# Gather stage: ScalarE copies a tick's transposes one tick later, and the convolutions and biases follow

## The chip, the cores and the metric

The kernel runs on one core of a Trainium2 chip. The metric is device time in microseconds (us) from launch to end of one execution; lower is better. The times given are of three runs, and one more execution was recorded by the hardware profiler.

The core has five engines with a queue each, worked through in the order in which the program lists their instructions: TensorE (PE in the profile, its weight loads PEld), VectorE (DVE), ScalarE (ACT), GpSimd (POOL) and SyncE (SP). They meet only through semaphores: an instruction waits until another engine's counter has reached a value.

## What is computed

Four layers, each a residual around a normalised input, on x of shape (8, 128, 64, 64) in float32. Layer 0 is a state-space block, Layer 1 passes rows and columns along in four directions (63 steps each), Layer 2 multiplies two convolutions, Layer 3 is a deformable convolution. The change lies in Layer 3:

```python
def corner(yi, xi, wgt):
    valid = (yi >= 0) & (yi < H) & (xi >= 0) & (xi < W)
    idx = jnp.clip(yi, 0, H - 1) * W + jnp.clip(xi, 0, W - 1)
    g = jax.vmap(lambda xb, ib: xb[:, ib])(xf, idx)
    return g * (wgt * valid)[:, None]
samp = corner(y0, x0, (1 - wy1) * (1 - wx1)) + corner(y0, x0 + 1, (1 - wy1) * wx1) + corner(y0 + 1, x0, wy1 * (1 - wx1)) + corner(y0 + 1, x0 + 1, wy1 * wx1)
samp = samp * mask[:, None]
out = jnp.einsum('bckhw,ock->bohw', samp, dcn_w.reshape(COUT, C, KK))
out = out + dcn_b[None, :, None, None]
```

For each of the 9 taps of each pixel, four neighbours (all 128 channels) are read at computed places, weighed and summed; a product over channels and taps then gives 128 output channels. After that come a normalisation over the whole batch and a leaky ReLU.

## The kernel before

**Stages.** Layer 0 runs first, over all eight images, with Layer 1's first half batch beside it. Then comes one long loop over ticks (lines 116 to 131) that puts together what is left of Layer 1, all of Layer 2 and Layer 3's gather. `finish` normalises and writes the result at the end.

**The loop.** Its order is written out by hand. A tick lists, in this order: one Layer 1 step's nine products (`next(step)`, L724, while Layer 1 lasts), `three.tick` (the gather), the step's sum on VectorE (the second `next(step)`, L732), Layer 2's events that are due (`plans`), and pieces of the `ahead` threads (loads of x into X at L700 to L701, residual adds at L761 to L764). An image has 96 ticks. Image b of the gather runs beside Layer 2 of image b+1; the gather has 8 x 96 = 768 ticks.

**A gather tick** takes one tile of 128 pixels (t, 32 to an image) and three taps (k0 = 0, 3 or 6). `gather` lists

- three indirect DMAs on GpSimd (L1105), one a tap, which fetch for each of the 128 pixels one row of 4 x 128 values,
- on ScalarE six weighings in place (L1116: three taps, neighbours 2 and 3), each with the pixel's weight as scale; every twelfth tick a copy of other weights comes ahead of them (L1095), which waits for VectorE's previous tick,
- on VectorE the weighing of neighbours 0 and 1 (L1121) and the sums. With `halves` 1 (the first 324 ticks) the four neighbours become one (L1125 to L1127), with `halves` 2 (the other 444, where the rows land in Layer 1's old buffer X) they become two (L1123) and TensorE adds the rest.

Landing buffers: six with `halves` 1 (`got`), ten with `halves` 2 (parts of X). A gather's DMAs wait until the transposes of the gather six or ten ticks earlier have read their buffer.

**What follows a gather** goes through `later(ticks, f)`, which puts a call on a list for the tick n + ticks; `tick` runs its `gather` first and then that tick's list, in the order in which the calls were put there.

- `turn`, one tick later: TensorE transposes the sums, pixels by channels into channels by pixels, by products with the identity (L1137: three taps, one or two each) into a PSUM tile `ps_s` with two buffers; ScalarE copies the tile (L1140) into half of a `samp` tile. Two tiles of pixels share a `samp`, which has four buffers.
- `convolve`, two ticks after the second pixel tile of a pair: three products of 256 columns (L1148) that accumulate into `ps_o`, which has one buffer. After the third group of taps, ScalarE adds the bias into `o_out` (L1156), and every second time
- `store`, two ticks on: SP writes `o_out` to DRAM (L1161) and VectorE takes its statistics (L1162).

A tick's ScalarE queue therefore reads: weighings of gather n, bias if one is due, copy of the transposes of gather n-1, then what Layer 2 lists in that tick (the main ones: L866 and L883 around t1, L856 and L900, L951 for tokens, L983 and L993 for offsets). Its TensorE queue reads: Layer 1's step (L724), convolution of gather n-2, transposes of gather n-1, then Layer 2's products (L876, L890, L948, L972). Its VectorE queue reads: L1121 and the sums of gather n, statistics, L732, Layer 2's work (L905 to L909).

Of the kernel before, what the change touches and what calls it, by code (L numbers as in the profile page):

```python
# [17 lines left out]
P = 128  # L18
# [9 lines left out]
KK = 9  # L28
# [1039 lines left out]
class Layer3:  # L1068
# [21 lines left out]
    def gather(self, b, t, k0, idx, wgt, halves):  # L1090
        nc, G3 = self.nc, self.G3
        if k0 == 0 and t % self.WT == 0:
            self.wps = self.prod[:, t // self.WT % 2, self.G3 * C : self.G3 * C + self.WT * KK * 2]
            self.wps = self.wps.rearrange("p (t k q) -> p t k q", k=KK, q=2)
            nc.scalar.copy(self.wps, wgt[:, t : t + self.WT, :, 0:2])  # L1095
        if t % self.PAIR == 0:
            self.samp[k0] = self.w2.tile([P, G3, self.PAIR * P], F32, name="samp", bufs=4)
        if halves == 1:
            got = self.w2.tile([P, G3, 4, C], F32, name="got", bufs=6)
        else:  # L1100
            n = self.n % (HW * NB2 // (G3 * 4 * C))
            got = self.more[:, n * G3 * 4 * C : (n + 1) * G3 * 4 * C].rearrange("p (k q c) -> p k q c", k=G3, q=4)
        tab = self.tables[b]
        for k in range(G3):
            nc.gpsimd.indirect_dma_start(  # L1105
                out=got[:, k, :, :].rearrange("p q c -> p (q c)"),
                out_offset=None,
                in_=tab,
                in_offset=bass.IndirectOffsetOnAxis(ap=idx[:, t, k0 + k : k0 + k + 1], axis=0),
            )  # L1110

        for k in range(G3):
            for q in (2, 3):
                nc.scalar.activation(  # L1116
                    got[:, k, q, :], got[:, k, q, :], AF.Identity, scale=wgt[:, t, k0 + k, q : q + 1]
                )
        prod = self.prod[:, :, 0 : G3 * C].rearrange("p q (k c) -> p k q c", c=C)
        w = self.wps[:, t % self.WT, k0 : k0 + G3, :]  # L1120
        nc.vector.tensor_mul(prod, got[:, :, 0:2, :], w.unsqueeze(3).to_broadcast([P, G3, 2, C]))  # L1121
        if halves == 2:
            nc.vector.tensor_add(got[:, :, 0:2, :], prod, got[:, :, 2:4, :])  # L1123
        else:
            nc.vector.tensor_add(prod[:, :, 0, :], prod[:, :, 0, :], got[:, :, 2, :])  # L1125
            nc.vector.tensor_add(got[:, :, 1, :], prod[:, :, 1, :], got[:, :, 3, :])
            nc.vector.tensor_add(got[:, :, 0, :], prod[:, :, 0, :], got[:, :, 1, :])  # L1127
        self.later(1, self.turn, halves, got, self.samp[k0], t % self.PAIR * P)
        if t % self.PAIR == self.PAIR - 1:
            self.later(2, self.convolve, b, t + 1 - self.PAIR, k0, self.samp[k0])  # L1130

    def turn(self, halves, got, samp, col):
        nc = self.nc
        ps = self.pp.tile([P, self.G3, P], F32, name="ps_s")
        for k in range(self.G3):
            for q in range(halves):
                nc.tensor.matmul(  # L1137
                    ps[:, k, :], lhsT=got[:, k, q, :], rhs=self.ident, start=(q == 0), stop=(q == halves - 1)
                )
        nc.scalar.copy(samp[:, :, col : col + P], ps)  # L1140

    def convolve(self, b, t0, k0, samp):
        nc, N2 = self.nc, self.PAIR * P
        if k0 == 0:
            self.ps_o = self.pp.tile([P, N2], F32, name="ps_o", bufs=1)
        ps = self.ps_o
        for k in range(k0, k0 + self.G3):
            nc.tensor.matmul(  # L1148
                ps, lhsT=self.dcn_w[:, k, :], rhs=samp[:, k - k0, :], start=(k == 0), stop=(k == KK - 1)
            )  # L1150
        if k0 + self.G3 < KK:
            return
        if t0 % 4 == 0:
            self.out = self.w2.tile([P, T], F32, name="o_out")
        o = self.out[:, t0 % 4 * P : t0 % 4 * P + N2]
        nc.scalar.activation(o, ps, AF.Identity, bias=self.dcn_b)  # L1156
        if t0 % 4:
            self.later(2, self.store, b, t0 // 4, self.out)
# [99 lines left out]
```

## Time and profile before

| | us |
|---|---|
| median of three runs | 7638.51 (7635.89 to 7647.05) |
| profiled execution | 8068.85 |
| its span, first to last instruction | 8066.5 |
| first and last weighing of the gather stage (start) | 3749.8 and 7891.9 |
| last step of Layer 1 | 5364 |
| busy in the span: TensorE, VectorE, ScalarE, GpSimd | 6262.5, 4469.1, 3505.2, 4114.6 |
| mean granted TensorE clock | 0.889 of full speed |

The profiled execution took 430 us longer than the median run. Line numbers are those of the kernel shown above. In a row of the profile, `out<-in` are the program's names of tiles, `x768` the number of instructions, then busy time and mean duration in ns, then the idle time of that engine just before these instructions and what ended most of it. A releaser `DMA name` is a transfer that landed, `issue` is idle time with no wait that the profile can name, `remote` a semaphore for which no record of this program accounts. TensorE's matmul ends are modelled by the profiler. A float32 product shows as two matmul records, so a set of transposes is 6 records with `halves` 1 and 12 with `halves` 2, and a convolution's three products are 6.

### The profile page before, as it was taken

Reading aid. Unit: us, or ns where it says so; the run is one execution under the profiler, and the core shown is the slowest. Engines: PE = TensorE matmul, PEld = TensorE weight load, DVE = VectorE, ACT = ScalarE, POOL = GpSimd, SP = SyncE. Lnnn points to the kernel's source line nnn. Section 1 sums busy time; section 2 is a strip of 40 time slices with the busy share of each in tenths; the row PEclk is TensorE's granted clock in tenths of the full one; section 3 lists DMA queues with packets and bytes.
Section 4 is the critical chain, followed back from the end, with each engine's and each line's share of the span. In section 5 each row is a group of like instructions: output and inputs, shape, how many; then the busy total and the mean of one; then the engine's idle time right before and its main releaser. Section 6 shows DMA issues by size and latency. Waiting matters only on the chain. (4 is left out here: it accounts for less than half of the span.)

```text
span 8066.5 us, 87137 instructions
## 1 busy us (share of the span) xinstructions
PE 6262.5 (78%) x30226; PEld 4059.5 (50%) x30226; DVE 4469.1 (55%) x5384; ACT 3505.2 (43%) x8218; POOL 4114.6 (51%) x3325
## 2 busy tenths in 40 slices
PE   6777878799999999538999999974467777676661
PEld 1222222255555556416777777753355555555551
DVE  4887887666666655111556545555445454454445
ACT  4554555433333331021444444444355555555453
POOL 3766666544444443111445444445565666666664
PEclk9887888799999999869999999987689888888785
DMA  1010110100000000131455455455566666666557
GB/s 41 26 44 26 38 36 28 35 12 24 21 19 18 17 14 9 54 118 51 150 174 160 155 163 158 152 163 172 170 201 194 207 195 201 192 199 201 177 176 259
DMA packets 333015, 897.77 MB, mean 111 GB/s; under 512 B 55464, under 2 KB 90544, under 8 KB 330528
## 3 DMA queue, kind: packets, MB, share of 16 engines
q0 software_dynamic: 184320, 604.13, 24.7%
q1 hardware_dynamic: 143648, 271.31, 10.3%
q10 hardware_dynamic: 4608, 16.78, 0.5%
q8 instruction: 239, 3.92, 0.2%
q14 instruction: 200, 1.64, 0.1%
HBM read 770.80 MB, written 121.21 MB: 111 GB/s over the span
## 5 line engine op out<-in xcount | busy, mean ns | idle before, releaser
L605 POOL TENSOR_TENSOR hb<-hb,bc 128x1024 f32<-128x1024 f32 x512 | 1216.4, 2379 | 1360.9 <-ACT carry L600 979.1
L1105 POOL DMA_INDIRECT X<-table,idx x1332 | 1272.1, 955 | 799.8 <-PE ps_s L1137 350.1
L1105 POOL DMA_INDIRECT got<-table,idx x972 | 930.0, 957 | 1083.8 <-ACT samp L1140 439.8
L594 DVE TENSOR_TENSOR_SCAN hb<-da,carry,u_ps 128x512 f32<-128x512 f32 x896 | 1098.0, 1267 | 275.8 <-PE ps_y L613 224.7
L576 ACT ACTIVATE da<-dt_ps 128x1024 f32<-128x1024 f32 x512 | 524.3, 1024 | 1316.0 <-PE dt_ps L559 1315.6
L1148 PE MATMUL ps_o<-samp,dcn_w 128*128 128x256 f32 x2304 | 676.4, 436 | 418.7 <-ACT samp L1140 224.0
L1137 PE MATMUL ps_s<-ident,X 128*128 128x128 f32 x5328 | 794.9, 308 | 241.2 <-DVE X L1123 144.7
L1140 ACT COPY samp<-ps_s 128x384 f32<-128x384 f32 x768 | 365.1, 475 | 1412.6 <-PE ps_s L1137 1033.7
L1123 DVE TENSOR_TENSOR X<-prod,X 128x768 f32<-128x768 f32 x444 | 425.2, 958 | 966.1 <-ACT X L1116 805.6
L1137 PEld LDWEIGHTS ps_s<-ident,X 128*128 128x128 f32 x5328 | 767.3, 221 | 303.1 <-DVE X L1123 161.7
L1116 ACT ACTIVATE X<-X,wgt 128x128 f32<-128x128 f32 x2664 | 826.1, 392 | 0.0
L559 PE MATMUL u_ps<-u,m_u 32*128 32x512 f32 x2048 | 639.3, 703 | 194.4 <-DVE hb L594 193.4
L1148 PEld LDWEIGHTS ps_o<-samp,dcn_w 128*128 128x128 f32 x2304 | 470.2, 214 | 554.2 <-ACT samp L1140 251.2
L583 DVE TENSOR_TENSOR u_ps<-u_ps,bc 128x1024 f32<-128x1024 f32 x512 | 625.2, 1221 | 182.1 <-PE dt_ps L559 165.3
L1116 ACT ACTIVATE got<-got,wgt 128x128 f32<-128x128 f32 x1944 | 611.2, 392 | 193.6 <-DMA got<-table,idx 189.9
L559 PE MATMUL dt_ps<-dt,m_dt 32*128 32x512 f32 x2048 | 642.5, 706 | 17.6 <-ACT da L576 17.6
L1121 DVE TENSOR_TENSOR prod<-X,prod 128x768 f32<-128x768 f32 x444 | 426.5, 961 | 117.4 <-ACT prod L1095 69.3
L1125 DVE TENSOR_TENSOR prod<-prod,got 128x384 f32<-128x384 f32 x324 | 183.6, 567 | 506.3 <-ACT got L1116 453.7
L559 PEld LDWEIGHTS u_ps<-u,m_u 32*128 32x128 f32 x2048 | 166.3, 198 | 553.2 <-DVE hb L594 365.9
L1121 DVE TENSOR_TENSOR prod<-got,prod 128x768 f32<-128x768 f32 x324 | 309.6, 955 | 145.7 <-DMA got<-table,idx 96.0
L1137 PE MATMUL ps_s<-ident,got 128*128 128x128 f32 x1944 | 296.1, 293 | 109.5 <-issue 47.6
L876 PE MATMUL ps_t<-xn,w 128*128 128x512 f32 (+4 forms) x688 | 317.3, 611 | 81.1 <-DVE t L907 56.6
(224 smaller groups left out, 10218.1 us busy)
## 6 DMA issues: line engine op xcount, KB each, us to landing
x<-x1d SPq DMA_DIRECT2D x128, 256.0 KB
table<-tok SPq DMA_DIRECT2D x128, 256.0 KB
X<-table,idx POOLq DMA_INDIRECT x1332
x<-x2d SPq DMA_DIRECT2D x48, 384.0 KB
x3h<-x3d SPq DMA_DIRECT2D x16, 1056.0 KB
x_st<-in_x SPq DMA_DIRECT2D x64, 256.0 KB
x_o<-in_x SPq DMA_DIRECT2D x64, 256.0 KB
x1d<-res SPq DMA_DIRECT2D x64, 256.0 KB
```

The source lines that it names most:

```text
L559: nc.tensor.matmul(ps[:, j, :], lhsT=mask[q, r].rearrange("p d n -> p (d n)"), rhs=S[c][src, h][q, :], start=True, stop=True,)
L576: nc.scalar.activation(da, steps[i]["dt"], AF.Exp)
L583: nc.vector.tensor_mul(st["bc"], st["bc"], s["bc", h][:, 0].unsqueeze(1).to_broadcast([P, 2, T]))
L594: nc.vector.tensor_tensor_scan(hb[:, j, :], st["da"][:, j, :], st["bc"][:, j, :], start, ALU.mult, ALU.add)
L605: nc.gpsimd.tensor_mul(hb, hb, S[c]["bc", h][:, 1].unsqueeze(1).to_broadcast([P, 2, T]))
L1105: nc.gpsimd.indirect_dma_start(out=got[:, k, :, :].rearrange("p q c -> p (q c)"), out_offset=None, in_=tab, in_offset=bass.IndirectOffsetO ...
L1116: nc.scalar.activation(got[:, k, q, :], got[:, k, q, :], AF.Identity, scale=wgt[:, t, k0 + k, q : q + 1])
L1121: nc.vector.tensor_mul(prod, got[:, :, 0:2, :], w.unsqueeze(3).to_broadcast([P, G3, 2, C]))
L1123: nc.vector.tensor_add(got[:, :, 0:2, :], prod, got[:, :, 2:4, :])
L1137: nc.tensor.matmul(ps[:, k, :], lhsT=got[:, k, q, :], rhs=self.ident, start=(q == 0), stop=(q == halves - 1))
L1140: nc.scalar.copy(samp[:, :, col : col + P], ps)
L1148: nc.tensor.matmul(ps, lhsT=self.dcn_w[:, k, :], rhs=samp[:, k - k0, :], start=(k == 0), stop=(k == KK - 1))
```

## The change

Three calls are put one tick later than what they follow:

- the copy of the transposes leaves `turn` and goes on the list of the next tick,
- `convolve` is called three ticks after its gather, not two,
- the bias with what follows it becomes a function `biased`, called one tick after the last group's convolution; `store` still comes two ticks after the bias.

In tick n ScalarE then has the weighings of gather n, a bias if one is due, and the copy of the transposes of gather n-2; TensorE has the convolution of gather n-3 and the transposes of gather n-1. No instruction is added or left out, and no buffer count changes.

```diff
         if t % self.PAIR == self.PAIR - 1:
-            self.later(2, self.convolve, b, t + 1 - self.PAIR, k0, self.samp[k0])
+            self.later(3, self.convolve, b, t + 1 - self.PAIR, k0, self.samp[k0])
 
     def turn(self, halves, got, samp, col):
...
-        nc.scalar.copy(samp[:, :, col : col + P], ps)
+        self.later(1, nc.scalar.copy, samp[:, :, col : col + P], ps)
 
     def convolve(self, b, t0, k0, samp):
...
-        if k0 + self.G3 < KK:
-            return
+        if k0 + self.G3 == KK:
+            self.later(1, self.biased, b, t0, ps)
+
+    def biased(self, b, t0, ps):
+        nc, N2 = self.nc, self.PAIR * P
         if t0 % 4 == 0:
             self.out = self.w2.tile([P, T], F32, name="o_out")
```

In the changed kernel the copies carry the line of `later` (L1088), since it is there that the call is made, and bias, store and statistics stand three lines further down (L1159, L1164, L1165).

## The prediction

> **What bounds the kernel now.** I read the page first, then the busy times of four stretches, the waits of TensorE in the first of them, and two short timelines. The page names the group that the change moves: 768 copies of transposes out of PSUM, in front of which ScalarE stands idle, mostly for the transposes of line 1137.
>
> ```profile
> span 8066.5 us, 87137 instructions
> ...
> L1140 ACT COPY samp<-ps_s 128x384 f32<-128x384 f32 x768 | 365.1, 475 | 1412.6 <-PE ps_s L1137 1033.7
> ```
>
> Idle time of an engine that is not the bound is free, so the question is who waits for ScalarE. The gather runs from about 3750 to 7897 us, and its stretches have different limits (windows, all engines):
>
> ```profile
> 3850.00:5380.00 1530.00, 1417.88 (x7177) 1180.77 (x7175) 848.12 (x1433) 694.50 (x2027) 723.71 (x757) 0.98 0.51 158
> 5380.00:5840.00 460.00, 213.78 (x728) 150.36 (x728) 233.12 (x382) 179.44 (x507) 254.62 (x247) 0.69 0.57 178
> 5840.00:7500.00 1660.00, 1189.09 (x6579) 949.00 (x6580) 809.00 (x957) 939.50 (x2788) 1012.03 (x1059) 0.88 0.64 197
> 7500.00:7840.00 340.00, 208.49 (x1129) 183.83 (x1128) 146.48 (x156) 172.46 (x545) 211.51 (x223) 0.81 0.59 176
> ```
>
> Stretch A (to 5380, Layer 1's steps beside the gather) is bound by TensorE: 1417.88 of 1530 us busy (93%), clock 0.98. Stretch R (to 5840, the residual adds) is bound by no engine; there ScalarE waits 181.4 us for landing gathers and GpSimd 100.1 us for x1d loads. Stretch B (Layer 3 with Layer 2, then alone) has TensorE at 72% and 61%. The first column after the length is TensorE, the fifth GpSimd, the sixth the granted clock.
>
> The gaps left on TensorE in A, by what ended them (us in total, times, longest):
>
> ```profile
> PE ps_l L724 <- DVE X L732: 36.8, 24, 3.8
> PE ps_tok L948 <- ACT tok L951: 16.9, 22, 2.1
> PE ps_o L1148 <- ACT samp L1140: 9.1, 16, 0.6
> PE ps_l L724 <- issue: 7.5, 4, 2.3
> ...
> PE ps_s L1137 <- issue: 4.0, 4, 1.2
> PE ps_t L876 <- DVE t L907: 3.9, 3, 1.5
> ...
> PE ps_s L1137 <- ACT got L1116: 2.0, 2, 1.6
> ```
>
> The largest looks like VectorE, but the timelines of ScalarE and TensorE at 5040 show where it starts:
>
> ```profile
> 5044.91 0.48 ACT L1140 COPY samp<-ps_s 128x384 f32<-128x384 f32 x1 [4.76 <-PE ps_s L1137]
> 5045.29 0.70 ACT L900 ACTIVATE ps_t<-t,w 128x512 f32<-128x512 f32 x1
> 5045.91 1.02 ACT L856 ACTIVATE xn<-x,norm 128x768 f32<-128x768 f32 x1
> 5046.83 1.85 ACT L1116 ACTIVATE got<-got,wgt 128x128 f32<-128x128 f32 x6
> ```
>
> ```profile
> 5043.99 0.83 PE L1137 MATMUL ps_s<-ident,got 128*128 128x128 f32 x6
> 5044.67 4.02 PE L724 MATMUL ps_l<-X,w_left 128*128 128x256 f32 x18
> ...
> 5051.22 1.10 PE L724 MATMUL ps_l<-X,w_left 128*128 128x256 f32 x4 [1.87 <-DVE X L732]
> ```
>
> ScalarE stood for 4.76 us at a copy whose transposes were queued behind a Layer 1 step. Its weighings therefore ended at 5048.68, VectorE's three sums and L732 followed at 5050.76, and TensorE lost 1.87 us. In B the same wait has a longer form (ScalarE):
>
> ```profile
> 7593.40 1.86 ACT L1116 ACTIVATE X<-X,wgt 128x128 f32<-128x128 f32 x6
> 7601.72 0.48 ACT L1140 COPY samp<-ps_s 128x384 f32<-128x384 f32 x1 [6.45 <-remote]
> ```
>
> The transposes that it waits for end at 7595.64 by the record, and "remote" means that no record tells what freed the copy.
>
> **What the Trainium skill says.** "Perfetto Trace Analysis", section "Tensor Engine Instruction (MATMUL, LD_WEIGHTS)": the recorded end of a matmul is an estimate and the semaphore follows only after PSUM's acknowledgement. The trace agrees: 6.08 us lie between that end and the copy. "TensorE: Matmul & The Clock Gate", section "Architectural detail": ScalarE and VectorE are strict first-in first-out, so a waiting copy holds every weighing behind it; the 4.76 us show that. The same page, "What's actually happening": the array's clock halves after about one idle window. The trace agrees: six convolution records take 1.56 us at 7583.46 and 2.93 us at 7602.25, after 6.61 us of pause. "Perfetto Trace Analysis", "GPSIMD Engine Instruction": time GpSimd by the spacing of starts. Here gathers start 1.26 us apart when nothing holds them (6164.50, 6165.75, 6167.01), not 0.95.
>
> **The change, part by part.**
>
> (1) Removed: the copy's wait. Before, in tick n, ScalarE does the six weighings of gather n, then copies the transposes of gather n-1, which TensorE does in that same tick n, behind Layer 1's step. After, it copies those of n-2, done a tick ago. The bias likewise waited for its own convolution (88.9 us on L1148 in A) and now takes one a tick old. In A the gaps that start at such a stop are L724 on L732 (36.8), convolution on copy (9.1), L724 "issue" (7.5), transposes (4.0 + 2.0), L876 on L907 (3.9): 63.3 us. The token and offset gaps (16.9, 7.0) stay: their copies still need products of their own tick, as does the t1 copy L883, which remains a stop in one tick of four. I take two thirds, 42 us; bounds 10 and 63. TensorE's work is unchanged, so a gap closed there is time saved.
>
> (2) R: at 5738.56 and 5742.29 copies wait 0.78 and 1.49 us for transposes on a chain that leads through L900, weighings, L909 and an x1d load to the next gather. All copies of R wait some 29 us (14.8 + 13.1 + 1.1). I take 20; bounds 0 and 40.
>
> (3) B: 444 ticks from 5845 to 7897 are 2052 us, 4.62 a tick. GpSimd needs 3 x 1.26 = 3.77 a tick, 1674 us, whatever ScalarE does; TensorE at full clock needs 12 x 0.125 for transposes and half of 1.56 for convolutions, 2.28, and in Layer 2's product ticks (4.46 + 2.69)/4 more, 4.07. The profiled execution took 8068.85 us, the median run 7638.51, 430 less. In B alone semaphore updates of TensorE come late or in bursts (three of one transposition 0.06 us apart at 6164.24, 1.4 us after its recorded end); before 3500 they come within 0.34 us. I choose to put most of the 430 there: 2052 - 1674 = 378 would account for it. Then timed runs of B already go at about GpSimd's pace, the product ticks (0.3 us slower than GpSimd) are absorbed by ten buffers of run-ahead, and unhooking ScalarE gains little. I take 8 us; bounds 0 and 140 (half of what would be there if the 430 were spread evenly: 2052 x 0.947 - 1674 = 269).
>
> (4) Added: transposes of gather g reuse the bank of g-2, whose copy now stands behind the weighings of g, and in one tick of six behind a bias. Queued behind that matmul on TensorE are the tick's Layer 2 products and the next step. But the transposes need VectorE's sum over those same weighings: 0.96 us in B, 0.57 + 0.56 + 0.56 in A. Copy and bias take 0.48 + 0.47. Covered; at most 0.1 us in 128 ticks, 13 us.
>
> (5) Moved at no cost, each hidden by slack in ticks: convolutions a tick later (samp has four buffers, next written three ticks after, as before); the bias before the next convolution group reuses ps_o (three ticks left of four); the store, its DMA on SP and its bn_stats two ticks later (still two ticks after the bias, so SP's queue, which carries the x1d loads behind it, gets no new wait). GpSimd's instructions keep order and waits. The last ticks drain through the same chain: 0 to 1 us.
>
> Sum: 42 + 20 + 8 = 70. On the profiled execution 8068.85 - 70 = 7999 (more if B's late updates are partly hidden by the slack); on the median 7638.5 - 70 = **7568**. I say 7570.
>
> **Rivals.**
> Bigger gain: the late updates of B are real in timed runs too. For: 711 us of idle before copies in B, 248.4 of it "remote". Against: the even match of 378 with 430. Then 62 + 135 = 197 less: 7440.
> No change: A's gaps reappear at the token, t1 and L732 waits that stay, R is held by its DMAs. For: ScalarE still stops at L883. Against: the 5040 timeline. 7635.
> Slower, by the clock: B at GpSimd's pace leaves TensorE 61% busy, and if the later convolutions and transposes bunch so that pauses outgrow the clock's window, work runs at half rate: 4.57 a tick against 3.77, 0.8 lost a tick. It decides once the clock of a stretch falls under 2.28/3.77 = 0.60 (now 0.81). With 112 such ticks: +90 - 62 = 28 over, 7666. For: the clock at 7602. Against: at GpSimd's pace the copy follows the weighings at once in both kernels, so TensorE's pattern hardly differs.
>
> **How the numbers follow.** Forecast 0.52, own range 7530 to 7612; bigger gain 0.15; no change 0.15; slower 0.18. Under 7460 lies about half of the bigger gain, over 7660 half of the slower case: range 7460 to 7660. 0.2% is 15 us, about what runs can tell (the three spread 11). Faster: 0.52 x 0.97 + 0.15 = 0.65; same 0.16; slower 0.19.
>
> **What would show it.** Step 1: copies (now under the line of the deferring helper) idle for transposes by under a fifth of 1033.7 us, and L724 on L732 in A under 12 us. Step 2: R near 440 us. Step 3: GpSimd spacing 1.26 over longer runs in B. Step 4: no wait of transposes on copies. I am wrong if A is not shorter by 10 us, or if the timed gain passes 140 us, which A and R cannot give.

## The result and the profile after

The changed kernel takes **7527.9 us** in the median of five runs (7518.93 to 7556.69), the kernel before 7638.51 beside it (7634.66 to 7647.68): 110.6 us less, a ratio of 0.9864, 95% interval 0.9848 to 0.9881. The prediction was 7570 us: the right sign, within its range (7460 to 7660), 2 us under the 7530 to 7612 that it gave its own forecast, and a gain of 110.6 us where 68.5 were forecast.

On some occasions this program takes about 7640 us before the change and on others about 8070, timed runs and recorded executions alike; the record of before shown above (8068.85 us) is of the second sort, that of after (7556.69 us) of the first, and gains are taken here only between runs of one sort.

The page of after has these rows. The copies now carry the line of the deferring helper.

```profile
span 7553.8 us, 87063 instructions
...
L1105 POOL DMA_INDIRECT X<-table,idx x1332 | 1273.0, 956 | 406.1 <-DMA X<-table,idx 164.7
...
L1137 PE MATMUL ps_s<-ident,X 128*128 128x128 f32 x5328 | 733.8, 292 | 263.1 <-ACT samp L1088 118.8
...
L1088 ACT COPY samp<-ps_s 128x384 f32<-128x384 f32 x768 | 357.0, 465 | 292.9 <-PE ps_s L1137 292.6
```

Same number of copies, 365.1 us of work before and 357.0 now, but ScalarE's idle time in front of them falls from 1412.6 to 292.9 us. Part of that is the other sort of run: put together from two records of the same sort as after, in which one part of the ticks has the code of before (see below), the copies wait 617.3 + 300.9 us for transposes, where after has 292.6. On the other hand TensorE now waits 118.8 us for copies before it may transpose, a wait that step 4 of the prediction had put at nearly nothing. Whether it costs anything is a question of place. The busy times by stretch (columns as before: length, TensorE, its loads, VectorE, ScalarE, GpSimd, granted clock, DMA share, GB/s):

```profile
3850.00:5380.00 1530.00, 1426.69 (x7335) 1199.11 (x7334) 911.76 (x1533) 732.41 (x2153) 788.05 (x818) 0.97 0.56 170
5380.00:5840.00 460.00, 272.85 (x1280) 199.98 (x1280) 236.09 (x355) 220.96 (x638) 267.31 (x269) 0.77 0.62 194
5840.00:7000.00 1160.00, 940.21 (x5698) 753.13 (x5699) 722.42 (x857) 820.23 (x2436) 879.83 (x920) 0.95 0.79 246
7000.00:7320.00 320.00, 213.52 (x1274) 191.01 (x1274) 167.35 (x177) 209.36 (x615) 242.54 (x255) 0.88 0.73 215
```

The first row can't be set against the row of before: Layer 1's stretch ends at 5258 us in this record, so that 122 us of the residual adds are in it. The experiments therefore count by ticks. The stretches after 5840 are those that the change was thought to leave alone: GpSimd there does 920 instructions in 1160 us and 255 in 320, one in 1.26 us, its pace with nothing in its way.

What is left of the waits beside Layer 1 (total us, times, longest), TensorE's first (3850 to 5268 us) and ScalarE's after (3850 to 5300):

```profile
PE ps_tok L948 <- ACT tok L951: 15.6, 22, 1.0
PE ps_l L724 <- DVE X L732: 9.8, 5, 3.7
```

```profile
ACT samp L1088 <- PE ps_s L1137: 281.7, 143, 9.7
ACT t L883 <- PE ps_t L876: 173.6, 24, 9.4
ACT tok L951 <- PE ps_tok L948: 149.1, 46, 8.6
```

L724 on L732 is down to 9.8 us (36.8 in the record shown above, 33.6 with the code of before in a record of the same sort). ScalarE still stops, most of all at the copies, 143 times, and longer than before at the t1 copies and the tokens, whose products are of their own tick. That those stops cost TensorE little is what the first of the two lists says: 15.6 us for tokens, and no line at all for convolutions on copies.

### The profile page after: what moved, and what is told of

It reads as the page before. It is cut to its first block, busy times and chain, and to the rows that moved or that the text cites. A ratio compares the mean times of both kernels' runs of the same rounds, so it can differ in the third digit from the quotient of the medians.

```text
span 7553.8 us, 87063 instructions
## 1 busy us (share of the span) xinstructions
PE 6101.3 (81%) x30226; PEld 3946.5 (52%) x30226; DVE 4478.6 (59%) x5384; ACT 3512.3 (46%) x8218; POOL 4113.4 (54%) x3325
## 5 line engine op out<-in xcount | busy, mean ns | idle before, releaser
L1116 ACT ACTIVATE X<-X,wgt 128x128 f32<-128x128 f32 x2664 | 867.3, 394 | 258.9 <-DMA X<-table,idx 254.2
L1137 PE MATMUL ps_s<-ident,X 128*128 128x128 f32 x5328 | 733.8, 292 | 263.1 <-ACT samp L1088 118.8
L1137 PEld LDWEIGHTS ps_s<-ident,X 128*128 128x128 f32 x5328 | 698.8, 205 | 327.0 <-ACT samp L1088 151.0
L1148 PE MATMUL ps_o<-samp,dcn_w 128*128 128x256 f32 x2304 | 614.2, 406 | 116.8 <-ACT samp L1088 116.0
L559 PE MATMUL dt_ps<-dt,m_dt 32*128 32x512 f32 x2048 | 648.2, 712 | 17.1 <-ACT da L576 17.0
L1148 PEld LDWEIGHTS ps_o<-samp,dcn_w 128*128 128x128 f32 x2304 | 446.3, 203 | 216.9 <-ACT samp L1088 144.6
L1088 ACT COPY samp<-ps_s 128x384 f32<-128x384 f32 x768 | 357.0, 465 | 292.9 <-PE ps_s L1137 292.6
L732 DVE SCALAR_TENSOR_TENSOR X<-ps_l,X 128x256 f32<-128x256 f32 x252 | 106.0, 420 | 501.4 <-PE ps_l L724 501.3
L732 DVE SCALAR_TENSOR_TENSOR X<-u_ps,X 128x256 f32<-128x256 f32 x252 | 106.9, 424 | 494.5 <-PE u_ps L724 492.6
```

Of the source, the lines that this page charges most:

```text
L559: nc.tensor.matmul(ps[:, j, :], lhsT=mask[q, r].rearrange("p d n -> p (d n)"), rhs=S[c][src, h][q, :], start=True, stop=True,)
L1088: self.late.setdefault(self.n + ticks, []).append(lambda: f(*args))
L1116: nc.scalar.activation(got[:, k, q, :], got[:, k, q, :], AF.Identity, scale=wgt[:, t, k0 + k, q : q + 1])
L1137: nc.tensor.matmul(ps[:, k, :], lhsT=got[:, k, q, :], rhs=self.ident, start=(q == 0), stop=(q == halves - 1))
L1148: nc.tensor.matmul(ps, lhsT=self.dcn_w[:, k, :], rhs=samp[:, k - k0, :], start=(k == 0), stop=(k == KK - 1))
```

## The experiments

The profile alone could not say in which stretch the gain lay, since the two records are of different sorts. Ticks are counted by the start of their six weighings; "beside Layer 1" is ticks 0 to 259, "residual adds" 259 to 324, "last part" 324 to 767. All of the table is worked out from the records in that way (us):

| record | first weighing | beside Layer 1 | residual adds | last part | span |
|---|---|---|---|---|---|
| before takes about 7640: | | | | | |
| first part changed (second run) | 3736.3 | 1495.1 | 445.2 | 1697.9 | 7551.8 |
| last part changed (second run) | 3736.0 | 1572.1 | 447.8 | 1671.0 | 7606.4 |
| after | 3761.9 | 1496.2 | 447.7 | 1669.8 | 7553.8 |
| before takes about 8070: | | | | | |
| before, shown above | 3749.8 | 1607.9 | 459.1 | 2073.5 | 8066.5 |
| before again | 3736.5 | 1614.4 | 468.4 | 2081.1 | 8076.0 |
| before, third | 3754.7 | 1606.7 | 462.2 | 2074.2 | 8076.4 |
| first part changed | 3719.6 | 1558.9 | 451.5 | 2091.4 | 7999.8 |
| last part changed | 3734.7 | 1609.9 | 467.9 | 2025.0 | 8015.9 |
| bias only | 3760.9 | 1607.6 | 464.2 | 2083.4 | 8093.4 |
| convolution only | 3717.1 | 1606.8 | 450.2 | 2043.7 | 7993.0 |
| after again | 3736.7 | 1540.5 | 450.4 | 1994.8 | 7896.3 |
| after, bias at once | 3734.0 | 1561.6 | 451.1 | 2000.6 | 7925.0 |
| after, loads ahead | 3678.8 | 1541.5 | 381.1 | 1998.4 | 7775.4 |
| after, loads ahead (second run) | 3721.0 | 1546.7 | 383.6 | 2001.1 | 7829.3 |

What a column is worth shows in records whose code is the same there. Where before takes about 7640 us, two such pairs agree within 1.2 us (1495.1 and 1496.2, 1671.0 and 1669.8). Where it takes about 8070, the stretch beside Layer 1 scatters by 8 us with the code of before (1606.7 to 1614.4) and by 18 with the change (1540.5 to 1558.9), the last part by 18 (2073.5 to 2091.4) and 30 (1994.8 to 2025.0); differences of that size between two such records tell nothing. The start scatters from 3717 to 3762 us without any edit to it.

**Before, once more.** No edit.

> The kernel before, unchanged, recorded a second time. Theory R (the late semaphore updates of TensorE in the last 444 ticks belong to that one recorded execution, and timed runs do not have them): the last 444 ticks take near 1674 us (3.77 a tick, GpSimd's spacing), the profiled execution comes near the median, 7600 to 7700 us, and copies no longer wait on releasers that the profile can't name. Theory K (they belong to the kernel as it was): again near 8070 us, 4.6 us a tick.

It took 8078.85 us, and the timed runs of before beside it 8077.85 (8048.41 to 8101.82, 35 runs). So the prediction and Theory R were wrong to take the 430 us for an effect of recording an execution: runs that are only timed have them too. Theory K, that they belong to the kernel, fails further on, where the same kernel takes 7636.53 us.

**The first part alone.** The change for the first 324 ticks, the code of before for the other 444.

```diff
+        d = int(halves == 1)
-        self.later(1, self.turn, halves, got, self.samp[k0], t % self.PAIR * P)
+        self.later(1, self.turn, halves, got, self.samp[k0], t % self.PAIR * P, d)
...
-            self.later(2, self.convolve, b, t + 1 - self.PAIR, k0, self.samp[k0])
+            self.later(2 + d, self.convolve, b, t + 1 - self.PAIR, k0, self.samp[k0], d)
...
-        nc.scalar.copy(samp[:, :, col : col + P], ps)
+        if d:
+            self.later(1, nc.scalar.copy, samp[:, :, col : col + P], ps)
+        else:
+            nc.scalar.copy(samp[:, :, col : col + P], ps)
...
-        if k0 + self.G3 < KK:
-            return
+        if k0 + self.G3 == KK:
+            if d:
+                self.later(1, self.biased, b, t0, ps)
+            else:
+                self.biased(b, t0, ps)
```

> The change in the first 324 ticks alone (one transpose a tap); the last 444 ticks as before. Theory A (the gain lies in the stretch beside Layer 1, where TensorE is the bound, with a little from the residual adds): 95 to 115 us under the kernel before, so 7525 to 7545 us, as fast as the whole change. Theory B (the last 444 ticks carry a good part of it): 40 to 70 us under.

**The last part alone.** The same edit with the other ticks chosen.

```diff
+        d = int(halves == 2)
```

> The change in the last 444 ticks alone; the first 324 as before. Theory A: within 15 us of the kernel before, as GpSimd issues a gather every 3.77 us whatever ScalarE does. Theory B: 40 us or more under it. In its profile, if the late updates come again, the last 444 ticks may still shrink: that would be the recording's doing.

The first part took 8025.68 us (ratio 0.9946, 0.9919 to 0.9972), 52 less than before beside it; the last part 8009.86 (0.9918, 0.9901 to 0.9935), 68 less. The absolute times can't be held against expectations written for the other sort of run; the split can. Where before takes about 8070 us, both parts gain; the intervals overlap, so which of them gains more is not shown.

**The bias alone**, one tick after its convolution; copies and convolutions where they were.

```diff
-        if k0 + self.G3 < KK:
-            return
+        if k0 + self.G3 == KK:
+            self.later(1, self.biased, b, t0, ps)
```

> The bias alone one tick later; copies and convolutions as before. Theory C (the copies' wait for transposes of the same tick is what holds the weighings back): 0 to 25 us under the kernel before, since the bias waits in one tick of six. Theory D (the bias, whose wait of 88.9 us for its convolution stands in front of a copy, does a share of its own): 40 us or more under.

8085.75 us, ratio 1.001 (0.9998 to 1.0022): no gain, at the lower end of what Theory C allows, and nothing of the 40 us of Theory D. ScalarE's longest waits beside Layer 1 (3850 to 5300 us), first of before (third record), then with the bias later:

```profile
ACT samp L1140 <- PE ps_s L1137: 548.5, 209, 7.7
ACT o_out L1156 <- PE ps_o L1148: 79.3, 28, 5.7
```

```profile
ACT samp L1140 <- PE ps_s L1137: 618.1, 195, 7.6
ACT t L883 <- PE ps_t L876: 53.8, 14, 6.5
```

The 79.3 us in front of biases are gone, and the copies right behind them in the queue wait 69.6 us more: one stop removed, the next one takes it over.

**The whole change again, and the whole change with the bias at once** (copies and convolutions a tick later, the bias again in its convolution's tick).

> The whole change, unchanged. The first set of runs showed two conditions: there the kernel before took 8078 us where it had taken 7638, with late semaphore updates of TensorE in every recorded execution. Theory S (the lateness belongs to the chip or its state, not to a kernel): where before takes near 8078 us, the whole change shows late updates too and takes about 8078 - 52 - 68 = 7958 us, the two parts' gains added; where before takes near 7638 us it takes 7528 again. Theory K (the change itself removes the lateness): near 7530 us in either case.

```diff
-            self.later(1, self.biased, b, t0, ps)
+            self.biased(b, t0, ps)
```

> Copies and convolutions a tick later, but the bias in the tick of its convolution, so that ScalarE waits for that convolution in one tick of six. Theory C (the copies are what matters): within 20 us of the whole change. Theory D (the bias matters together with the copies, since one stop in six ticks pins ScalarE to TensorE again): 30 us or more slower than the whole change.

The whole change took 7906.77 us where before took 8057.68 (ratio 0.981, 0.9771 to 0.9849), so it doesn't take the longer times away (Theory K), but gains 151 us among them. Theory S had the sign, but its 7958 us, the two parts' gains of 52 and 68 added, was 51 too high; the parts were timed on another occasion, and where the rest comes from is not known.

With the bias at once it took 7940.27 us (0.9852, 0.9805 to 0.9899): 33.5 us more than the whole change, as Theory D had it. In the records 21 of them lie beside Layer 1, which is hardly more than the scatter there; the waits are plainer. ScalarE's beside Layer 1 (3850 to 5240 us), first for the whole change, then with the bias at once:

```profile
ACT samp L1088 <- PE ps_s L1137: 237.8, 116, 9.6
...
ACT o_out L1159 <- PE ps_o L1148: 52.1, 26, 4.0
```

```profile
ACT o_out L1159 <- PE ps_o L1148: 230.4, 34, 11.1
ACT samp L1088 <- PE ps_s L1137: 134.2, 55, 9.2
```

The stops at biases hold 178 us more, and those at copies 104 less: the stop moves to the next instruction in ScalarE's queue that wants a product of its own tick. So the bias is worth nothing alone and some 34 us together with the copies, by four runs of each; it was not left out where before takes about 7640 us. The intervals of the two ratios overlap; of the times on that occasion, the longest of the whole change (7913.51) lies just under the shortest with the bias at once (7915.42).

**The convolution alone**, a tick later.

```diff
-            self.later(2, self.convolve, b, t + 1 - self.PAIR, k0, self.samp[k0])
+            self.later(3, self.convolve, b, t + 1 - self.PAIR, k0, self.samp[k0])
```

> The convolutions alone a tick later; copies and biases stay where they were, so ScalarE still waits for each transpose of its own tick. Theory C (the copies' wait is what costs): within 15 us of the kernel before. Theory E (it is TensorE's own wait for the copy just made, in front of a convolution, that costs; a tick more of distance removes it): 50 us or more under before.

8020.88 us against 8067.09 (ratio 0.9939, 0.9923 to 0.9955): 46 less. Theory C's 15 us were missed by far, and Theory E's 50 nearly reached, yet not where TensorE is the bound: none of it lies beside Layer 1 (1606.8 against 1606.7). The last part is 30.5 shorter, which is more than the 18 by which before's code scatters there, the residual adds 12, the rest is within the scatter of the start. Beside Layer 1, then, it takes the later copies, with the biases, to gain anything (copies that are late while convolutions stay can't be had, since a convolution would then stand ahead of its copy in the tick's list). In the last part the convolution of gather n-2 needs a copy made one tick before, and there TensorE's signals come late on these occasions (last section), which a tick more covers; that this is the reason is argued, not shown, and the kernel was not timed where before takes about 7640 us.

**Before, third time**, beside the convolution alone.

> The kernel before once more. Should this fall where before takes near 7638 us, Theory A expects of its record: no late updates, the last 444 ticks at GpSimd's 3.77 us a tick (near 1674 us, as with the change), the first 259 ticks near 1595 us against 1496 with the change, and the 65 ticks of the residual adds near 460. Theory B expects the last 444 ticks at 4.0 us a tick or more. Where before takes near 8070 us it tells only that this repeats.

8078.66 us; the timed runs beside it 8067.09 (8034.22 to 8119.74, 20 runs), so it tells only that this repeats. It gives the record that the last reading used.

**The first part again**, on an occasion where before took 7636.53 us (7627.91 to 7677.77, 7 runs).

> The change in the first 324 ticks only, beside before; the point is to see it where before takes about 7638 us, the time that the result was compared with. There: Theory P (all of the gain lies beside Layer 1 and the residual adds, the last 444 ticks already go at GpSimd's pace) expects the whole gain, 7520 to 7540 us, and in its record the last 444 ticks, whose code is that of before, at 3.77 us a tick (1665 to 1680 us), TensorE's updates almost none late. Theory Q (half of the gain lies in the last 444 ticks) expects 7575 to 7590 us and those ticks at 3.85 to 3.95 us. Where before takes about 8070 us again, it repeats the earlier run: 8010 to 8035 us, and the question stays open.

7558.23 us (ratio 0.989, 0.984 to 0.9941): 78 less, between the two theories. Its last 444 ticks, which run the code of before, take 1697.9 us, against 1669.8 in after: 28 us. Theory P had them equal, Theory Q some 36 to 80 between them. GpSimd's waits over those ticks (5680 to 7370 us) say where the 28 are, first of this kernel, then of after (5710 to 7370):

```profile
POOL X L1105 <- issue: 128.6, 422, 0.3
POOL X L1105 <- DMA X<-table,idx: 125.8, 412, 0.6
POOL X L1105 <- PE ps_s L1138: 93.1, 216, 4.6
```

```profile
POOL X L1105 <- DMA X<-table,idx: 164.1, 538, 0.4
POOL X L1105 <- issue: 121.3, 398, 0.3
POOL X L1105 <- PE ps_s L1137: 47.9, 157, 0.3
```

Every gather has some 0.3 us of idle ahead of it, whatever it is booked to; that is the pace of 1.26 us. What counts is the longest: 4.6 us for transposes (L1138 in this kernel) against 0.3 after the change. Worked out from the starts, the time over 1.26 us between gathers sums to 33 us here and to 3 in after, and most of it falls on a few gathers in each image, while Layer 2's products (L876) run. Such a place, on ScalarE, on TensorE and on GpSimd:

```profile
6394.15 0.48 ACT L1144 COPY samp<-ps_s 128x384 f32<-128x384 f32 x1 [0.30 <-PE ps_s L1138]
...
6398.44 0.59 ACT L883 COPY t<-ps_t 128x512 f32<-128x512 f32 x1 [3.62 <-PE ps_t L876]
6398.92 1.86 ACT L1116 ACTIVATE X<-X,wgt 128x128 f32<-128x128 f32 x6
```

```profile
6393.94 4.46 PE L876 MATMUL ps_t<-xn,w 128*128 128x512 f32 x10
6398.24 1.46 PE L1152 MATMUL ps_o<-samp,dcn_w 128*128 128x256 f32 x6
6399.53 1.50 PE L1138 MATMUL ps_s<-ident,X 128*128 128x128 f32 x12
```

```profile
6396.43 0.96 POOL L1105 DMA_INDIRECT X<-table,idx  x1 [0.30 <-issue]
6400.41 0.95 POOL L1105 DMA_INDIRECT X<-table,idx  x1 [3.03 <-PE ps_s L1138]
```

Layer 2's products hold TensorE for 4.46 us, ScalarE's queue stands at L883 meanwhile, the transposes that free a landing buffer come late, and the ten buffers have run out: GpSimd stops for 3.03 us. The first 28 ticks of an image with such products take 130.1 to 132.1 us in this record, 4.7 a tick, and 119.0 to 120.2 in after, 4.3 a tick (worked out from the starts, three images each); with 4.3 the buffers suffice. Whether the later copy or the later convolution does it was not separated on such an occasion: in the last part convolutions wait for copies too, 93.0 us in this record and 59.5 in after (5800 to 7300 us).

**The last part again**, where before took 7643.48 us (7615.57 to 7672.99, 19 runs).

> The change in the last 444 ticks only; its first 324 ticks have the code of before, so where before takes about 7638 us its record shows what before does there. Theory P2 (about 80 us of the gain lie in the first 324 ticks and about 28 in the last 444, as the run of the first part alone left it) expects 7600 to 7618 us, the last 444 ticks at 1665 to 1675 us (before's code took 1697.9 there), and the first 324 ticks at 2010 to 2035 us together against 1943.9 after the change, most of it in the 259 ticks beside Layer 1. If step 1 of the prediction was right about the record and the rest of the gain lies elsewhere, those 259 ticks take about 1540 us and the run 7590 us or less. Where before takes about 8070 us it repeats the earlier run: 7990 to 8030 us.

7609.02 us (ratio 0.9959, 0.9944 to 0.9975): 34 less, and the last part at 1671.0 us. Theory P2 held in all it named, the first 324 ticks (2019.9 us) included. The two parts add up: 78.3 + 34.5 = 112.8 against 110.6 for the whole. Its record also gives the first 324 ticks of before's code on such an occasion: 1572.1 us beside Layer 1, 76 more than after, and 447.8 for the residual adds, against 447.7. Of TensorE's waits beside Layer 1 (3850 to 5300 us) it has:

```profile
PE ps_l L724 <- DVE X L732: 33.6, 22, 2.5
PE ps_tok L948 <- ACT tok L951: 14.6, 21, 0.7
PE ps_o L1152 <- ACT samp L1144: 9.1, 16, 0.6
```

and of ScalarE's over the same time:

```profile
ACT samp L1144 <- PE ps_s L1138: 571.0, 229, 7.7
ACT o_out L1166 <- PE ps_o L1152: 92.7, 34, 5.7
ACT t L883 <- PE ps_t L876: 79.3, 21, 6.7
ACT tok L951 <- PE ps_tok L948: 15.7, 21, 0.7
```

Against after, the copies' 571.0 us have halved to 281.7, and the t1 copies and tokens have taken up most of the rest (173.6 and 149.1). Over ticks 0 to 259 ScalarE is idle for 867 us here and for 798 in after, a fall of 69 us in a stretch that is 76 shorter: it has not become busier, for TensorE bounds the stretch and ScalarE waits for it in either order. What has gone is that TensorE in turn waits for something that ScalarE was late with (L724 on L732 33.6 to 9.8, convolutions on copies 9.1 to none).

**Loads ahead.** The whole change, and in the residual add each piece's load is issued one piece earlier, since the change had hardly moved the residual adds in any record.

```diff
+    def load(g):
+        x = pool.tile([P, T], F32, name="x1", bufs=3)
+        nc.sync.dma_start(x, x1d[b][:, g * T : (g + 1) * T])
+        return x
+
+    ahead = load(0)
...
-        x = pool.tile([P, T], F32, name="x1", bufs=3)
-        nc.sync.dma_start(x, x1d[b][:, s])
+        x, ahead = ahead, load(g + 1) if g + 1 < NCH else None
```

> The whole change, and in the residual adds each x1d load issued one piece ahead, so that GpSimd no longer stands in front of a gather until the load has landed. If the 448 us of the residual stretch are bound by that wait (GpSimd 100 us for the loads): 60 to 120 us under the whole change. If they are bound by the landing of gathers or by Layer 2's chain: within 20 us of it.

> The whole change, and the load of each residual add's piece issued one piece ahead. Theory R (beside the residual adds the kernel is held by GpSimd's own wait for those loads, so that no order on ScalarE can shorten it: those 65 ticks took 447.8, 445.2 and 447.7 us in three records of different code) expects them at 375 to 385 us as before, and the start about 55 us earlier, since the same adds stand ahead of the gather: where before takes about 7638 us, 7395 to 7425 us against 7528 of the change alone. Rival (the load's own traffic only moves into the gather's landing) expects 7500 us or more. Where before takes about 8070 us it repeats the earlier run, 7775 to 7800 us.

Where before took 8067.09 us it took 7785.17 (ratio 0.965, 0.9595 to 0.9705); the second time, beside 8050.77, 7764.66 (0.9646, 0.9624 to 0.9668), 10 us under what was expected for such an occasion. The whole change alone stood at 0.981, so this version beats both kernels. GpSimd's waits beside the residual adds, of the whole change run again (5280 to 5730 us) and of the first of these runs (5250 to 5650):

```profile
POOL x L762 <- DMA x<-x1d: 121.3, 10, 32.4
```

```profile
POOL x L767 <- DMA x<-x1d: 8.9, 2, 5.7
```

The second of these records has 42.3 us of that wait. The stretch shrinks from 450.4 to 381.1 and 383.6 us, and Theory R's 375 to 385 were met: GpSimd's own wait for those loads, in front of its gathers, held it. By the ratios the edit is worth some 129 us beyond the whole change, a little over the 60 to 120 expected. The start was expected 55 us earlier: 3678.8 in the first record, but 3721.0 in the second, which is inside the scatter; that record is of the slowest of its five runs (7831.43 us, the others 7753 to 7770). What the edit is worth ahead of the gather stays open, and it was not timed where before takes about 7640 us.

## Why the prediction was right in sign and too small

**Step 1 (forecast 42 us of 63.3; measured 76).** The place and the wait were right, the size was not. From 1572.1 to 1496.2 us TensorE does the same work. Of the 76 us, the idle gaps give 45.5 (92.7 to 47.2, worked out from the records), so two thirds of the gaps was a fair choice. The other 30 us come out of *busy* time, 1479.5 to 1449.0, which the step had as unchanged. Worked out from the records they divide so:

- Some 5 us are 30 of 7434 records fewer, because work shifts by a tick, at 0.1 to 0.2 us each.
- Some 12 us are the clock. The granted clock stood at half for 41.0 us of the stretch with before's code and for 17.1 after (0.987 and 0.994 on average), with 38.4 and 14.3 us of work in it, which would take about half as long at the full clock (one Layer 1 record starts 402 ns after another there and 212 ns elsewhere). In each of these stretches of half clock, 11 before and 3 after, TensorE had idled for 48 to 100% of the 3.4 us ahead. A gap closed thus gave time twice, and the prediction, which had reckoned with the clock in its slower rival, put it at nothing here.
- Some 9 us are short stops behind transposes. From the start of a transposition record to the start of the next record, idle gaps taken off, the sums are 185.9 us for 1548 records before and 176.2 for 1542 after, 120 and 114 ns a record, most of it where a Layer 1 step or a convolution follows. The prediction quoted the Trainium skill on exactly that end ("Perfetto Trace Analysis", section "Tensor Engine Instruction (MATMUL, LD_WEIGHTS)"), which the page calls an estimate, and then summed idle gaps alone. A stop that is shorter than what is left of the estimated end is booked as busy; that this is what the 9 us are is inferred.
- The last 4 us are not assigned.

**Step 2 (forecast 20, measured 0).** The copies' wait in that stretch was there (35.0 us from 5270 to 5740 in the last part's second record, which has before's code there) and went (0.3 in after), but 447.8 and 447.7 us for the whole stretch say that it was beside the path: GpSimd waits for the x1d loads, 133.5 us there and 120.9 in after. The chain that the step followed leads through such a load to the next gather; the step took the load as given and looked at ScalarE. (Where before takes about 8070 us the stretch does get shorter, some 450 us where before's records have 459.1 to 468.4, and that with the convolutions alone as well.) Its test, "near 440", was met by 447.7 for no reason of the step's.

**Step 3 (forecast 8, measured 28).** That timed runs of this part go at about GpSimd's pace was right: 1697.9 us before, 3.83 a tick, where 2052 less 378 was expected, that is 3.77. Put together from the two records, before's code spans 3736.0 + 1572.1 + 447.8 + 1697.9 and 179.6 after the last weighing, 7633.4 us; of the 433 by which the record shown above is longer, 376 lie in this part, as the step put it, though not because an execution was recorded: the pace was right for a reason that was wrong. Nor did late updates come "in B alone": 88 of the 423 in that record lie ahead of it, and the stretch beside Layer 1 is longer there too (1607.9 against 1572.1). The 6.08 us that the prediction set beside PSUM's acknowledgement are such a late update; in the records of the shorter sort all but two come within 0.4 us of the recorded end. What failed is that product ticks, put at 4.07 us, "are absorbed by ten buffers of run-ahead": with before's code they take 4.7 us, the buffers run out, and GpSimd lost 33 us, most of it there. After the change they take 4.3, and 99% of its gathers start within 1.30 us of each other.

**Step 4 (0 to 13 us).** The wait of transposes on copies came, 118.8 us, against "no wait of transposes on copies". It costs nothing that can be seen: 105.3 us of it lie between 5800 and 7300 us, in the last part, which goes at 3.77 us a tick with it.

**Step 5** stood: no new stop at samp, ps_o or the store shows among the waits.

The tests: the copies' idle was to fall under a fifth of 1033.7 us, 207; it is 292.6. L724 on L732 under 12: 9.8. The sum is 76 + 0 + 28 = 104 in the records, 110.6 in the medians, for 42 + 20 + 8 = 70. That 20 us too many in one step stood against 54 too few in the other two is luck, and brought the total nearer than the steps were. The rival of no change and the slower one by the clock fell (0.95 and 0.88 granted in the last part, where 0.60 was its point). The bigger gain is true of the other sort of run: where TensorE's signals come late, the change is worth 151 us (7906.77 against 8057.68), by the records some 80 of them in the last part; the rival had named 197.

## What to carry to other kernels

An engine that works through its queue in order should find its operands made a step earlier; delay all instructions of that kind together, since the stop moves to the next one that still wants a product of its own step (the bias alone brought nothing, left out it cost 34 us). To price stops on TensorE, count besides the idle gaps the half clock that follows some of them, and the stops that are booked as busy time. An engine that is not the bound may stand idle as long as before and yet hold nobody up. And before counting a wait as time, follow the chain one step further, to see whether a transfer would have held the same instruction anyway.

## What the runs showed of the hardware

The same program took about 8070 us on some occasions and 7640 on others, and it is not the chip: one and the same chip gave 8057.68 us for before at one time and 7643.48 at a later one. In the three records of before of the long sort, of 5339 TensorE instructions that signal by the main semaphore, only 4813 to 4824 updates appear, and 406 to 483 of them come over 0.4 us after the recorded end, most of them in the last part; in the records of the short sort none is missing and two are late. The whole change in the long sort has 817 late ones and is yet 151 us faster, so the count alone doesn't set the time. With before's code in the long sort the gathers of the last part start over 1.30 us apart in a quarter of the cases, at the same 0.95 us each. What brings the one or the other about was not found.

Beside Layer 1 the granted clock fell to half in pieces of 3.4 or 6.8 us, in the two records named above each time after 3.4 us of which TensorE had idled half or more; it did not take 3.4 us without any work.
